# Shorter memory runs, weight reloads one step earlier, and another spread of the second batch's norm stages in a cross-attention and mixture-of-experts kernel

## The chip, the cores and the metric

The kernel runs on one core of one Trainium2 chip. The metric is the time of one execution on the device in microseconds (us). An execution is one launch that computes the whole block for four batches.

The core has a matrix engine (TensorE, in the profile PE for its matmuls and PEld for its weight loads), three engines for elementwise work (VectorE, in the profile DVE; ScalarE, ACT; GpSimd, POOL) and SyncE (SP), which in this kernel only issues data transfers. Transfers (DMAs) are issued on two queues here: those of SP, and those of POOL. Both are carried by the same 16 DMA engines. Each engine works through its own list of instructions in order, so an instruction that waits holds back whatever stands behind it on its engine.

## The reference

Inputs are `x` (4 batches, 512 rows, 512 features) and a context of 256 features for each row. Cut to what matters, and for each batch:

```
ln  = layernorm(x)
att = softmax((ctx Wq + bq)(ctx Wk + bk)^T)          # 512 x 512
x1  = x + (ln^T att)^T                               # cross attention
hs  = layernorm(x1)                                  # input of the block, and its residual
h   = rmsnorm(hs) * ln1
for 16 heads of 128: q, k, v = h wq, h wk, h wv
    a = softmax(q k^T / sqrt(128), causal) v
x2  = hs + concat(a) wo
t   = rmsnorm(x2) * ln2
top 6 of 16 experts for each row, weights from softmax(t gate^T)
out = x1 + x2 + sum over the 6 experts(silu(t eg) * (t eu)) ed + shared expert(t)
```

Each expert is 352 wide, the shared expert 704. All is float32. The kernel keeps the accuracy by splitting each float32 operand into two half-precision parts (a high one and a low one) and doing three half-precision matmuls for each product.

## The kernel before

**Cross attention** of a batch is written as a Python generator, `xattn(b)`. It yields after each small stage, and `step(b, n)` lets it run `n` stages on. There are 21 stages for batches 1 to 3: one for the two projections, eight for the energies and their softmax (two for each of four row tiles), and three for each of four row tiles that multiply the attention with the normalized input (`xm`, a group of 12 matmuls), normalize twice, and put the result transposed into `hT[b]`. These last twelve are the *norm stages*. The transposes are done by DMAs that SP issues (`flip`, line 91); in this document such a DMA is called a flip.

**Self attention** runs over a list of (batch, head) pairs, 64 in all, one head a step (the loop over `n`). The list goes through groups of two heads; from the third group on, batch 0 and batch 1 alternate with the same group (later batch 1 with 2, and 2 with 3), so that one set of weights serves two batches. In a step the queries and keys of a head are computed (`queries`), every second step also the values of its group (`values`), then the scores and their softmax (`scores`), and for the head of the step before the product with the values (`attend`, matmuls named `av`). `attend` reads a tile `pt` that four flips fill. `project` multiplies a finished group with its part of the output weights. The first batch is prepared ahead of the loop, and the first nine stages of batch 1 too. The twelve norm stages of batch 1 are done two a step in steps 0 to 5, and batches 2 and 3 are brought later by one or two stages a step. The first head of batch 1 stands at step 6.

**Weights.** `fetch` brings the weights of a head (`wqk`) or group (`wv`, `wo`), 512 KB each in split form. The first time, float32 weights are loaded into a staging tile, split by ScalarE and VectorE (`split`, lines 73 and 74), and the split form is written to a scratch tensor in memory (`wqk_d` and so on, line 429). Later uses load it from there (line 414): these are the *reloads*, 40 in all, issued by POOL at the place in the program where the weights are used. Two buffers of each kind exist, and `held` keeps a tile for the partner batch that uses it next.

**Routing.** When a batch is finished, `route1` to `route3` compute its expert choice. Rows are then sent to memory by scatters (line 467), indirect DMAs of 256 KB on POOL, a few in each step. `pace` holds them back: it puts a one-element copy on POOL that reads what a previous step's `attend` made, and the scatters stand behind that copy.

**The order** of instructions on each engine is not the program's. A planner simulates the program with costs of its own and writes out a list for each engine. Manual dependencies (`after`) and `pin` fix parts of that order. A moved instruction can thus move others on all engines.

After the attention come the shared expert and the 16 experts; the change has no part of its own there, except that `residual` loads `r_d`, and that the shared weights and the padding rows are brought with other shapes.

**Memory layout.** A tile has 128 partitions. In the kernel before, each scratch tensor and each prepared input has the partition as its first index, so that one DMA moves for each partition one unbroken run: 4 KB for a weight, 2 KB for a row of `x1_d`, `hid_d` or `r_d` (8 KB where four rows are loaded at once).

Of the kernel before, what the change touches and what calls it, by code (L numbers as in the profile page):

```python
# [17 lines left out]
P = 128  # L18
# [29 lines left out]
PS = 4096.0  # L48
GS = 8.0
LAG = 1  # L50
MLAG = 2
# [4 lines left out]
def xattn_moe_block_kernel(ctx: ExitStack, tc: tile.TileContext, x, xT, ctxT, wqkx, bqk, ln1, ln2,  # L56
# [23 lines left out]
    def mm3(o, terms, start=True, stop=True, hold=None):  # L80
        n = len(terms)
        for j, (lh, ll, rh, rl) in enumerate(terms):
            ins = nc.tensor.matmul(o, lh, rh, start=start and j == 0, stop=False)  # L83
            if hold and j == 0:
                after(ins, hold)
            nc.tensor.matmul(o, lh, rl, start=False, stop=False)  # L86
            ins = nc.tensor.matmul(o, ll, rh, start=False, stop=stop and j == n - 1)  # L87
        return ins

    def flip(o, i):  # L90
# [40 lines left out]

    hid_d = [dram.tile([P, NT, D], F32, name=f"hid_d{b}") for b in range(B)]
    x1_d = [dram.tile([P, NT, D], F32, name=f"x1_d{b}") for b in range(B)]
    wqk_d = [dram.tile([P, 2048], F16, name=f"wqk_d{h}") for h in range(H)]
    wv_d = [dram.tile([P, 8 * GW], F16, name=f"wv_d{g}") for g in range(G)]
    wo_d = [dram.tile([P, 2 * HG * D], F16, name=f"wo_d{g}") for g in range(G)]
    xs_d = dram.tile([ROWS, 2 * D], F16, name="xs_d")
    r_d = [dram.tile([P, NT, D], F32, name=f"r_d{b}") for b in range(B)]
    y_d = dram.tile([OFFS[E], D], F32, name="y_d")
# [39 lines left out]
    def ctx_load(b):  # L179
        t = stg.tile([P, 1024], F32, tag="st", name="ct32").rearrange("p (c s) -> p c s", c=CC)  # L180
        feed(b).dma_start(t, ctxT[b])
        return t

# [20 lines left out]
    def xattn(b):  # L204
        ct32 = ctx_load(b) if b else ct0

        def turned(j):
            t = (stg if b else wg).tile([P, 1024], F32, tag="st" if b else "wo", name="xT32")
            feed(b).dma_start(t, xT[b, j])
            return t  # L210
# [5 lines left out]
        if b == 0:  # L216
            nc.sync.dma_start(ln1b, ln1.partition_broadcast(P))
            for nm, src in (("wqk0", wqk[0]), ("wv0", wv[0])):
                t = vp.tile([P, NT, 2, GW], F16, tag="vt", name=f"{nm}_st")
                early_st[nm] = t.rearrange("p t a d -> p (t a d)").bitcast(F32)  # L220
                nc.sync.dma_start(early_st[nm], src)
        ctp = ap_.tile([P, 2, CC, S], F16, tag="lnp", name="ctp")
# [109 lines left out]
        for t in range(NT):  # L332
# [5 lines left out]
            q = nc.gpsimd if b else nc.sync  # L338
            q.dma_start(x1_d[b][:, t, :], xv)
            st = asm.tile([P, 6], F32, name="st")  # L340
# [14 lines left out]
            if b >= 2:  # L355
                q.dma_start(hid_d[b][:, t, :], hd)
            if stop == "A":
# [36 lines left out]
    def shared_pool():  # L394
        actx.close()
        sp = ctx.enter_context(tc.tile_pool(name="sp", bufs=1, side="right", reuse_waits="tile"))
        shx["p"] = ctx.enter_context(tc.tile_pool(name="ac0", bufs=1, side="right", reuse_waits="tile"))
        shw = shx["w"] = sp.tile([P, 2, C * 2 * SI], F16, name="shw")
        sdw = shx["d"] = sp.tile([P, 2, 6 * D], F16, name="sdw")
        for j in range(0, C * 2 * SI, 1024):  # L400
            pieces.append((shw[:, :, j:min(j + 1024, C * 2 * SI)], sgu[:, j:min(j + 1024, C * 2 * SI)]))
        for j in range(0, 6 * D, 1024):
            pieces.append((sdw[:, :, j:j + 1024], sd[:, j:j + 1024]))

    held, partner, seen = {}, {}, set()

    def fetch(b, g, pool, tag, n, src, scr, nm):
        if held.get(nm, (None,))[0] == (b, g):
            return held.pop(nm)[1]
        w = pool.tile([P, 2, n], F16, tag=tag, name=f"{nm}_{b}")  # L410
        if (b, g) in partner:
            held[nm] = partner[b, g], w
        if nm in seen:
            nc.gpsimd.dma_start(w.rearrange("p a n -> p (a n)"), scr)
            return w
        seen.add(nm)
        first = nm in early_st
        if first:
            st_ = early_st[nm]
        else:  # L420
            st_ = stg.tile([P, 1024], F32, tag="st", name=f"{nm}_st")
            q = nc.sync if nm == "wqk1" else nc.gpsimd
            ins = q.dma_start(st_[:, :n], src)
            if nm == "wqk1":
                after(ins, zz["hT", 0])
        for j, ins in enumerate(split(w[:, 0], w[:, 1], st_[:, :n], WS)):
            if first:
                after(ins, zz["nb"] if j else zz["calm"][0])
        ins = (nc.sync if nm == "wqk0" else nc.gpsimd).dma_start(scr, w.rearrange("p a n -> p (a n)"))
        if nm != "wqk0":  # L430
            zz["pad"] = ins
        if nm == "wqk0":
            after(ins, zz["ptp", 0])
        return w
# [5 lines left out]
    def shared_weights():  # L440
# [6 lines left out]
        if pieces:  # L447
            dst, src = pieces.pop(0)
            n = src.shape[1]
            st_ = stg.tile([P, 1024], F32, tag="st", name="shst")[:, :n]  # L450
            pin(nc.gpsimd.dma_start(st_, src))
            loaded.append((dst, st_))
# [3 lines left out]
    def pace(src):  # L456
        ins = nc.gpsimd.tensor_copy(mark, src)
        if "rrs" in zz:
            after(ins, zz["rrs"])
        for s in scats:  # L460
# [18 lines left out]
    def pad_rows(e):  # L479
        r = e * T + CAP + 1 - 3 * HB  # L480
        dst = xs_d[r:r + 3 * HB, :].rearrange("r d -> (r d)").rearrange("(p a n) -> p a n", p=P, a=2)
        src = causal[:, :S - P].bitcast(F16).unsqueeze(1).to_broadcast([P, 2, 2 * (S - P)])
        after(nc.gpsimd.dma_start(dst, src), zz["pad"])

    def route1(b, x2):
# [20 lines left out]
        if b == B - 1:  # L506
            pace(h2p[0:1, D:D + 1])
            for t, x1t in enumerate(x1s):
                after(nc.gpsimd.tensor_tensor(x1t, x1t, x2[:, t, :], ALU.add), scats[0])
                nc.gpsimd.dma_start(r_d[b][:, t, :], x1t)  # L510

    x1s = []

    def last_residual(b):
        for t, (pool, tag) in enumerate([(he, "pn3"), (he, "pn3"), (xp, "x1t"), (xp, "h2")]):
            x1t = pool.tile([P, D], F32, tag=tag, name="x1t", **({} if pool is he else dict(bufs=1)))
            nc.gpsimd.dma_start(x1t, x1_d[b][:, t, :])
            x1s.append(x1t)
# [3 lines left out]
    def rest_step():  # L522
        if rest:
            b, t, x2 = rest.pop(0)
            x1t = xp.tile([P, D], F32, tag="x1t", name="x1t", bufs=1)
            ins = nc.gpsimd.dma_start(x1t, x1_d[b][:, t, :])
            for s in scats[-1:]:
                after(ins, s)
            nc.gpsimd.tensor_tensor(x1t, x1t, x2[:, t, :], ALU.add)
            nc.gpsimd.dma_start(r_d[b][:, t, :], x1t)  # L530

# [91 lines left out]
    def values(b, g):  # L623
        hb = hT[b]
        wvt = fetch(b, g, wg, "wv", C * GW, wv[g], wv_d[g], f"wv{g}").rearrange("p a (c d) -> p a c d", c=C)
        vt = vts[b, g] = vp.tile([P, NT, 2, GW], F16, tag="vt", name="vt")
# [10 lines left out]
    def queries(b, h):  # L637
        hb = hT[b]
        wt = fetch(b, h // HG, wp, "wqk", 1024, wqk[h], wqk_d[h], f"wqk{h}").rearrange("p l (a c d) -> p l a c d", a=2, c=C)
        qk = qks[b, h] = []  # L640
# [54 lines left out]
    def project(b, g):  # L695
        if b not in x2s:
            x2s[b] = x2p.tile([P, NT, D], F32, tag="x2", name="x2")
            nc.gpsimd.dma_start(x2s[b], hid_d[b])
        ao, x2 = aos[b, g], x2s[b]
        wot = fetch(b, g, wg, "wo", HG * D, wo[g], wo_d[g], f"wo{g}").rearrange("p a (c d) -> p a c d", c=HG)  # L700
        for t in range(NT):
# [7 lines left out]
    def residual(b):  # L709
        if b not in accs:  # L710
            pool = hpool if b else shx["p"]
            accs[b] = pool.tile([P, NT, D], F32, tag="hT", name=f"acc{b}")
            nc.sync.dma_start(accs[b], r_d[b])
        return accs[b]
# [65 lines left out]
    for n in range(NH + LAG + 1):  # L780
        if n < NH:
# [13 lines left out]
            for p in parts:  # L795
                for _ in p:
                    pass
        m = n - LAG
        if n == NH:
# [18 lines left out]
        if 0 <= m < NH:  # L818
            b, h = heads[m]
            attend(b, h)  # L820
            if h % HG == HG - 1:
                ready.append((b, h // HG))
        if n in agenda and n < NH:
            b = agenda[n]
# [12 lines left out]
        if n < 6:  # L837
            step(1, 2)
        else:
# [397 lines left out]
def host_layout(i):  # L1237
# [5 lines left out]
    r["x"] = f["x"]  # L1243
    r["xT"] = f["x"].transpose(0, 2, 1).reshape(B, 2, 2, P, S).transpose(0, 1, 3, 2, 4).reshape(B, 2, P, 2 * S)
    r["ctxT"] = f["ctx_1024"].transpose(0, 2, 1).reshape(B, CC, P, S).transpose(0, 2, 1, 3)
    r["wqkx"] = np.stack([_pc(f["L0_xattn_Wq"].T, CC), _pc(f["L0_xattn_Wk"].T, CC)], 1)
# [6 lines left out]
    for n in ("wqk", "wv", "wo"):  # L1253
        r[n] = r[n].reshape(r[n].shape[0], P, -1)
    r["gate"] = _pc(g("gate_w").T, C).reshape(P, C * E)
# [10 lines left out]
    cols.append(np.concatenate([sg[:, :, 5 * P:], su[:, :, 5 * P:]], 2).reshape(P, C * P))  # L1266
    r["sgu"] = np.concatenate(cols, 1)
    r["sd"] = _pc(np.pad(g("sd_w").T, ((0, 6 * P - SI), (0, 0))), 6).reshape(P, 6 * D)
    return {k: np.ascontiguousarray(v) for k, v in r.items()}
# [24 lines left out]
```

## Time and profile before

| what | us |
|---|---|
| median of 3 runs | 1773.08 |
| lowest and highest run | 1766.79 and 1774.21 |
| profiled execution | 1762.41 |
| its span, first to last instruction | 1760.7 |
| PE busy in it | 1708.6 (97%) |
| DVE, ACT, POOL busy | 1116.2, 829.3, 485.1 |

The mean clock granted to TensorE is 0.993 of full speed. A profile comes from one execution. In its rows a name like `wqk<-wqk_d` says what is written and what is read; L414 is line 414 of the kernel; `x20` is a count. A value in square brackets behind an instruction is the time for which its engine had been idle before it, and what released it. "Busy" of PE means that matmuls are in the array or on their way; they overlap, so the time from start to start is a better measure than the length of one.

### The profile page before, as it was taken

Reading aid. Unit: us, or ns where it says so; the run is one execution under the profiler, and the core shown is the slowest. Engines: PE = TensorE matmul, PEld = TensorE weight load, DVE = VectorE, ACT = ScalarE, POOL = GpSimd, SP = SyncE. Lnnn points to the kernel's source line nnn. Section 1 sums busy time; section 2 is a strip of 40 time slices with the busy share of each in tenths; the row PEclk is TensorE's granted clock in tenths of the full one; section 3 lists DMA queues with packets and bytes.
Section 4 is the critical chain, followed back from the end, with each engine's and each line's share of the span. In section 5 each row is a group of like instructions: output and inputs, shape, how many; then the busy total and the mean of one; then the engine's idle time right before and its main releaser. Section 6 shows DMA issues by size and latency. Waiting matters only on the chain. (4 is left out here: it accounts for less than half of the span.)

```text
span 1760.7 us, 27659 instructions
## 1 busy us (share of the span) xinstructions
PE 1708.6 (97%) x9919; PEld 932.9 (53%) x9919; DVE 1116.2 (63%) x2766; ACT 829.3 (47%) x1711; POOL 485.1 (28%) x614
## 2 busy tenths in 40 slices
PE   7899999999998999999999999999999999999998
PEld 3555556565654555556555544455555555555553
DVE  6787877787785676776667647544434344356755
ACT  4565655565643545454445422344544445444431
POOL 5524212240255242121113454300000000034654
PEclk9999999999999999999999999999999999999999
DMA  7787867575687787556547653755554546589866
GB/s 246 181 205 184 225 150 192 122 196 118 138 183 187 163 177 179 120 120 118 111 104 132 140 155 128 247 173 148 150 173 137 154 143 163 154 228 254 221 198 213
DMA packets 392212, 296.24 MB, mean 168 GB/s; under 512 B 334880, under 2 KB 335136, under 8 KB 391296
## 3 DMA queue, kind: packets, MB, share of 16 engines
q1 hardware_dynamic: 353360, 159.87, 39.9%
q0 software_dynamic: 38704, 134.51, 25.5%
q8 instruction: 80, 1.31, 0.3%
q14 instruction: 68, 0.56, 0.1%
HBM read 124.81 MB, written 88.94 MB: 121 GB/s over the span
## 5 line engine op out<-in xcount | busy, mean ns | idle before, releaser
L1169 POOL DMA_INDIRECT yg<-y_d,yrc x96 | 109.9, 1145 | 505.2 <-PE u L87 426.0
L673 ACT ACTIVATE pe<-pe,bnm 128x128 f32<-128x128 f32 (+3 forms) x256 | 142.5, 557 | 161.5 <-DVE bnm L671 161.3
L83 PE MATMUL qk<-hT,wqk 128*128 128x512 f16 (+1 forms) x520 | 196.4, 378 | 9.1 <-DMA wqk<-wqk_d 5.5
L86 PE MATMUL qk<-hT,wqk 128*128 128x512 f16 (+1 forms) x520 | 196.5, 378 | 0.0
L87 PE MATMUL qk<-hT,wqk 128*128 128x512 f16 (+1 forms) x520 | 196.3, 377 | 0.0
L74 DVE SCALAR_TENSOR_TENSOR pn<-pe,brc,pn 128x128 f16<-128x128 f32 (+3 forms) x256 | 148.1, 590 | 21.3 <-ACT pn L73 18.0
L671 DVE CUSTOM_DVE_ANT_0 pe<-sc,causal 128x128 f32<-128x128 f32 (+3 forms) x256 | 117.0, 485 | 66.9 <-PE sc L668 65.9
L73 ACT ACTIVATE pn<-pe,brc 128x128 f16<-128x128 f32 (+3 forms) x256 | 133.5, 553 | 34.1 <-ACT pe L673 17.8
L83 PE MATMUL v<-wv,hT 128*128 128x256 f16 x512 | 139.8, 273 | 0.9 <-DMA hT<-hh 0.9
L87 PE MATMUL v<-wv,hT 128*128 128x256 f16 x512 | 139.7, 273 | 0.0
L86 PE MATMUL v<-wv,hT 128*128 128x256 f16 x512 | 139.7, 273 | 0.0
L83 PE MATMUL g<-xT,wt 128*128 128x384 f16 (+2 forms) x384 | 127.3, 331 | 0.0
L86 PE MATMUL g<-xT,wt 128*128 128x384 f16 (+2 forms) x384 | 127.2, 331 | 0.0
L87 PE MATMUL g<-xT,wt 128*128 128x384 f16 (+2 forms) x384 | 127.2, 331 | 0.0
L1058 ACT ACTIVATE hT_e<-hf 128x384 f16<-128x384 f32 (+3 forms) x96 | 51.1, 532 | 133.6 <-DVE hf L1072 133.2
L83 PE MATMUL y<-dt,hT_e 128*128 128x512 f16 (+1 forms) x288 | 109.4, 380 | 0.0
L87 PE MATMUL y<-dt,hT_e 128*128 128x512 f16 (+1 forms) x288 | 108.9, 378 | 0.0
L86 PE MATMUL y<-dt,hT_e 128*128 128x512 f16 (+1 forms) x288 | 108.9, 378 | 0.0
L73 ACT ACTIVATE qkt<-qk 128x512 f16<-128x512 f32 x128 | 75.1, 587 | 70.7 <-PE qk L87 70.5
L705 DVE SCALAR_TENSOR_TENSOR x<-wo,x 128x512 f32<-128x512 f32 x128 | 87.2, 685 | 33.3 <-PE wo L87 32.9
L467 POOL DMA_INDIRECT xs_d<-h2p,slotu x96 | 98.7, 1028 | 28.3 <-issue 27.1
L74 DVE SCALAR_TENSOR_TENSOR qkt<-qk,qkt 128x512 f16<-128x512 f32 x128 | 87.5, 684 | 18.3 <-ACT qkt L73 15.2
(333 smaller groups left out, 4041.5 us busy)
## 6 DMA issues: line engine op xcount, KB each, us to landing
y_d<-yt SPq DMA_DIRECT2D x96, 256.0 KB, 2.8
est<-in_ew_dram SPq DMA_DIRECT2D x32, 704.0 KB, 6.2
est<-in_ed_dram SPq DMA_DIRECT2D x16, 768.0 KB, 4.7
wqk<-wqk_d POOLq DMA_DIRECT2D x20, 512.0 KB, 5.0
wqk_d<-wqk POOLq DMA_DIRECT2D x15, 512.0 KB, 4.0
wqk_st<-in_wqk_dram POOLq DMA_DIRECT2D x14, 512.0 KB, 6.4
xs_d<-causal POOLq DMA_DIRECT2D x16, 384.0 KB, 5.6
wv<-wv_d POOLq DMA_DIRECT2D x10, 512.0 KB, 5.7
```

The costliest lines, as they stand in the source:

```text
L73: return (nc.scalar.activation(hi, src, AF.Copy, scale=scale), nc.vector.scalar_tensor_tensor(lo, src, scale, hi, ALU.mult, ALU.subtract))
L74: nc.vector.scalar_tensor_tensor(lo, src, scale, hi, ALU.mult, ALU.subtract))
L83: ins = nc.tensor.matmul(o, lh, rh, start=start and j == 0, stop=False)
L86: nc.tensor.matmul(o, lh, rl, start=False, stop=False)
L87: ins = nc.tensor.matmul(o, ll, rh, start=False, stop=stop and j == n - 1)
L467: ins = nc.gpsimd.indirect_dma_start(out=xs_d, out_offset=bass.IndirectOffsetOnAxis(ap=slotu[:, tt, k:k + 1], axis=0), in_=h2ps[tt], in_of ...
L671: nc.vector.tensor_tensor_reduce(pe, ps[:, :w], causal[:, S - w:], -1.0, 3e38, ALU.add, ALU.min, nm)
L673: nc.scalar.activation(pe, pe, AF.Exp, bias=nm, scale=-1.0, accum_out=sm)
L705: nc.vector.scalar_tensor_tensor(x2[:, t, :], ps, 1.0 / (VS * WS), x2[:, t, :], ALU.mult, ALU.add)
L1058: nc.scalar.activation(hT[:R, ic, :w], hf, AF.Copy)
L1169: nc.gpsimd.indirect_dma_start(out=yg, out_offset=None, in_=src, in_offset=bass.IndirectOffsetOnAxis(ap=idx[:, tt, k:k + 1], axis=0))
```

## The change

Three things change, and no arithmetic does.

1. *Runs.* A helper `runs` issues a DMA in blocks, and tensors in memory are laid out block first, then partition. Split weights are moved in runs of 1 KB (512 half-precision numbers), rows of `x1_d`, `hid_d` and `r_d` in runs of 1 KB (`RUN` = 256 float32 numbers), and staged weights and the transposed inputs in runs of 2 KB. The prepared inputs are laid out anew to match. The padding rows are written in 384 runs of 1 KB instead of 256 of 1.5 KB.
2. *Reloads.* `fetch` gets a mode `early`, which issues a reload and keeps the tile in `soon`. It is called for the next step's `wqk` and, where a group begins, `wv`, behind the queries of this step, and for `wo` behind the `attend` that finishes a group. A first load is not done early. `pace` puts its copy behind the last such reload on POOL.
3. *Norm stages.* In steps 0 to 5 `step(1, 2)` becomes `step(1, 3 * (n > 0))`: none in step 0, then three a step, so that the twelve are done by step 4.

The core of the diff (renamings and the other uses of `runs` are left out):

```diff
+RUN = 256
...
+    def runs(q, o, i):
+        blocks = [v.rearrange("p (q n) -> p q n", q=w.shape[0]) if len(v.shape) == 2 else v.rearrange("q p n -> p q n")
+                  for v, w in ((o, i), (i, o))]
+        return q.dma_start(*blocks)
...
-    hid_d = [dram.tile([P, NT, D], F32, name=f"hid_d{b}") for b in range(B)]
-    x1_d = [dram.tile([P, NT, D], F32, name=f"x1_d{b}") for b in range(B)]
-    wqk_d = [dram.tile([P, 2048], F16, name=f"wqk_d{h}") for h in range(H)]
+    def rows_d(nm, b):
+        return dram.tile([NT, D // RUN, P, RUN], F32, name=f"{nm}{b}")
+
+    def weights_d(nm, i):
+        return dram.tile([2048 // (2 * RUN), P, 2 * RUN], F16, name=f"{nm}{i}")
+
+    hid_d, x1_d, r_d = ([rows_d(nm, b) for b in range(B)] for nm in ("hid_d", "x1_d", "r_d"))
+    wqk_d = [weights_d("wqk_d", h) for h in range(H)]
...
+    def wqk_of(b, h, early=False):
+        return fetch(b, h // HG, wp, "wqk", 1024, wqk[h], wqk_d[h], f"wqk{h}", early)
...
-    def fetch(b, g, pool, tag, n, src, scr, nm):
+    def fetch(b, g, pool, tag, n, src, scr, nm, early=False):
+        if early and nm not in seen or soon.get(nm) and early:
+            return
         if held.get(nm, (None,))[0] == (b, g):
-            return held.pop(nm)[1]
-        w = pool.tile([P, 2, n], F16, tag=tag, name=f"{nm}_{b}")
+            return None if early else held.pop(nm)[1]
+        w = soon.pop(nm, None)
+        if w is None:
+            w = pool.tile([P, 2, n], F16, tag=tag, name=f"{nm}_{b}")
+            if nm in seen:
+                zz["load"] = runs(nc.gpsimd, w.rearrange("p a n -> p (a n)"), scr)
+        if early:
+            soon[nm] = w
+            return
         if (b, g) in partner:
             held[nm] = partner[b, g], w
         if nm in seen:
-            nc.gpsimd.dma_start(w.rearrange("p a n -> p (a n)"), scr)
             return w
...
     def pace(src):
         ins = nc.gpsimd.tensor_copy(mark, src)
-        if "rrs" in zz:
-            after(ins, zz["rrs"])
+        for k in ("rrs", "load"):
+            if k in zz:
+                after(ins, zz[k])
...
+            if n + 1 < NH:
+                b, h = heads[n + 1]
+                wqk_of(b, h, True)
+                if h % HG == 0:
+                    wv_of(b, h // HG, True)
...
             if h % HG == HG - 1:
                 ready.append((b, h // HG))
+                wo_of(b, h // HG, True)
...
         if n < 6:
-            step(1, 2)
+            step(1, 3 * (n > 0))
```

## The prediction

> **What bounds the kernel now.** The header and the first part of the page come first: TensorE is busy nearly all the time.
>
> ```profile
> span 1760.7 us, 27659 instructions
> PE 1708.6 (97%) x9919; PEld 932.9 (53%) x9919; DVE 1116.2 (63%) x2766; ACT 829.3 (47%) x1711; POOL 485.1 (28%) x614
> q1 hardware_dynamic: 353360, 159.87, 39.9%
> q0 software_dynamic: 38704, 134.51, 25.5%
> ```
>
> The timeline shows back-to-back 512-column matmuls starting every 0.215 us. Summing columns at that rate over all matmuls gives 1655 us; the rest of the span is pauses of PE, half-rate stretches after them, and small change. So nothing in this diff can win more than what PE waits for. The waits of PE say what that is:
>
> ```profile
> PE av L83 <- DMA pt<-pn: 16.9, 10, 3.9
> PE xm L83 <- DMA ptp<-pn: 9.8, 2, 5.8
> PE qk L83 <- DMA wqk<-wqk_d: 5.5, 1, 5.5
> PE qk L83 <- DMA hT<-hh: 3.6, 2, 3.2
> ```
>
> Columns: us in total, times, longest. Three rows are DMA transposes ("flips", issued by SP); one is a weight reload, once, 5.5 us. Its place, from the PE and POOL timelines:
>
> ```profile
> 538.93 0.96 POOL L467 DMA_INDIRECT xs_d<-h2p,slotu  x1 [0.30 <-issue]
> 539.89 0.60 POOL L414 DMA_DIRECT2D wqk<-wqk_d  x1
> ...
> 542.92 0.38 PE L668 MATMUL sc<-qkt,qkt 128*128 128x512 f16 x1
> 548.81 0.61 PE L83 MATMUL qk<-hT,wqk 128*128 128x512 f16 x1 [5.51 <-DMA wqk<-wqk_d]
> 549.21 0.63 PE L86 MATMUL qk<-hT,wqk 128*128 128x512 f16 x1
> 549.64 0.63 PE L87 MATMUL qk<-hT,wqk 128*128 128x512 f16 x1
> ```
>
> The reload was issued behind ten scatters of 256 KB, 3 us before its use. After the pause matmuls start 0.43 us apart until 554.0, i.e. at half rate for 5.2 us: 2.5 us more. The place costs **8.0 us**.
>
> **The change, part by part.** No matmul, activation or vector operation is added; counts are equal, order and DMA shapes differ.
>
> *Reloads a step ahead.* In the built order of POOL nearly all reloads keep their place within three instructions (wqk0, wqk1, wqk2, wqk9 and wqk11 move by one to three). One moves far: wqk3, the one above, from behind ten scatters to ahead of them and of the eight L611 multiplies, 17 to 20 us earlier (520 to 523). Its buffer was last read by the queries at 517.9 to 523, so POOL may hold up to 3 us there; behind it stand the L611 products and the scatters, for which nobody waits within the step. So wqk3 is there in time and the 5.5 us go. What is late next is a flip. In the new order PE does 4 matmuls with wqk3 and then `attend` (L83 av), which needs all four flips of its pt. They were issued here, and the issue view gives the landing:
>
> ```profile
> 537.82 1.58 SPq L91 DMA_TRANSPOSE pt<-pn  x1
> 539.80 1.43 SPq L91 DMA_TRANSPOSE pt<-pn  x1
> ...
> pt<-pn SPq DMA_TRANSPOSE x1, 9.3
> ```
>
> 9.3 us after 539.80 is 549.1: before the change `av` started at 550.92 and so never showed this wait. Now PE comes to it at 544.0. Upper bound of the pause: 5.1 us. But the reload's 512 KB no longer run beside this flip (8 rows of 4 KB per DMA engine, at some 0.16 us each in the input stream of 12 to 20 us: 1.3 us), and the flip itself is 64 packets per engine at 32 ns (from q1's 3424 packets in 61.5% of 11 us at 604 to 615): 2 us alone, so 2 us is the lower bound of its landing. I take a pause of 2 to 3 us.
>
> Here the clock decides. Row: after the 2.48 us pause at 585.43 the matmuls go on at 0.38 us (full rate), after 5.51 us they take 0.63. The Trainium skill, "TensorE: Matmul & The Clock Gate", Part 1, says that the clock halves after an idle window of about 3.4 us and needs about 3.4 us of work to return. It speaks against the change: a 4 us flip wait keeps the half rate. Then PE resumes at 548 and half rate till 553.2, a gain of 1 to 2 us; by the rule's recovery, 1.7 us of loss instead of the 2.5 measured, about 2.5. With a pause under 3.4 us the gain is 8.0 - 2 = **6.0 us**. I take 6.0; bounds 1 and 8.
>
> *Norm stages of batch 1.* `step(1, 2)` six times becomes nothing, then three at a time. The first xm of batch 1 leaves the place where PE waited 3.97 us at 72.4 to 76.6 (with the half rate after it 5.6 us). Next behind it in the new order are 6 scores matmuls, which need score banks that VectorE empties. VectorE and ScalarE stand in the same order as before up to there, and were held by the same flip:
>
> ```profile
> 71.89 0.72 ACT L73 ACTIVATE pn<-pm,rc 128x512 f16<-128x512 f32 x1 [4.63 <-DMA ptp<-pn]
> 72.64 0.75 DVE L74 SCALAR_TENSOR_TENSOR pn<-pm,rc,pn 128x512 f16<-128x512 f32 x1 [4.75 <-ACT pn L73]
> ...
> 74.78 0.55 DVE L671 CUSTOM_DVE_ANT_0 pe<-sc,causal 128x384 f32<-128x384 f32 x1
> ```
>
> The bank is free at 75.3 instead of 76.6: 1.3 us; work moved in front of `av` (14 qk and 9 sc matmuls, 4 us, against 12 xm, 2.6) cannot all be used, as wqk3's split ends at 81.3. I take **1.5 us**; bounds 0 and 5.6. The last batch-1 stage is a step earlier by count, but in the PE order its fourth xm stands 10 us ahead of the first batch-1 queries as before, so the 0.39 us hT wait at 138.9 is worth at most **0.5**. SP issues the same flips: the first two hT1 flips now stand behind four more pt flips of 1.3 us each, the third two places earlier; on POOL the first x1_d store of batch 1 stands behind six weight DMAs (3.5 us). Nobody on PE waits for either before the hT wait named.
>
> *Short runs.* Weight scratch (31 stores, 40 reloads) goes from 128 rows of 4 KB to 512 of 1 KB; staged inputs to 256 of 2 KB; x1, hid, r rows to 256 of 1 KB. POOL's price by form:
>
> ```profile
> L483 POOL DMA_DIRECT2D xs_d<-causal x16 | 11.7, 768 | 0.0
> L414 POOL DMA_DIRECT2D wqk<-wqk_d x20 | 11.0, 551 | 58.1 <-PE qk L87 56.6 <-PE rk L597 1.5
> L215 POOL DMA_DIRECT2D xt<-in_x_dram x2 | 1.6, 812 | 0.3 <-POOL x L354 0.3
> ```
>
> These are 256, 128 and 512 rows. So +0.26 us for each of 71 scratch DMAs, +0.2 for some 100 others: 40 us on an engine busy 485 of 1760, hidden by its idle time; without that cover, at a scatter burst, 0.5 us.
>
> The DMA engines: "DMA: Bandwidth & Descriptors", section "Why small descriptors are slow (HBM only)", gives about 3 cycles over 32-byte beats for each packet: 4 KB is 131 cycles, four 1 KB 140, +7%. The row: 993 packets of mean 2.5 KB in the input stream took 107 ns, 1384 of mean 2.3 KB, 299 of them flips' 256 bytes, 96 ns; split, this is about 163 ns for 4 KB and 88 for 2 KB, +8% already at 2 KB, and an estimated +23% at 1 KB. 71 x 1.3 us x 23% is 21 us of all engines, by the rule 6.5. It shows only where a flip or a load is waited for. First 25 us: 3.7 MB of input in 2 KB rows instead of 4, at saturated engines, +0.7 us on PE. Ten pt pauses and the flips around 67 us: 0.2 to 0.3 us each where scratch traffic runs beside, 2. In the other direction finer runs may let a flip alternate with 1 KB instead of 4 KB; but 256 rows of 2 KB (x1t and r_d, 604 to 615) appear as 160 packets, so rows are joined up to 4 KB and I count this little. Bounds -6 (flip waits a fifth shorter) to +12 (every pause of 31 us a third longer, some loads late); I take **+1.0** net.
>
> *Redrawn pauses.* Order on PE changes nearly everywhere to the end of attention. Pauses at 585, 643, 672, 921, 970 came with a load beside the flip; a load issued sooner takes up to 1.3 us off. I take -2 for all, bounds -6 and +6.
>
> **Sum**: -6.0 - 1.5 - 0.5 + 1.0 - 2.0 = -9.0. The profiled execution took 1762.4 (span 1760.7), the runs 1766.8 to 1774.2 with median 1773.1, 0.6% above it. I carry the difference over: **1764**.
>
> **Rivals.** (1) *The flip takes the reload's place*: pause of 4 to 5 us at 544, half rate stays. For it: 9.3 us of landing. Gain there 1.5, all in all -3.5, with runs at +2.5: 1771, no change to be told. (2) *Short runs make it slower*: in the first 600 us DMA share reaches 1.04 (80 to 100), flips are waited for by ScalarE (4.63 us above) and PE. If scratch and staging rows take a third longer, each of the 15 flip pauses (31 us) grows by 1 us or more, and staged weights, waited for by ScalarE 1.3 us at 87.9, hold its queue at some ten of 31 loads by 0.5: +17 against -6 gained, 1784. It decides once a 512 KB reload lands over 2 us later than now (5.0). Against it: half the DMA time is idle. (3) *Flips alternate per run*: flip waits a fifth shorter, -6 more: 1757. (4) The reload doesn't move is ruled out by the built order.
>
> **How the numbers follow.** Measurement tells about 0.5% (8.9 us) from no change. Stated sum and rival 3 together 0.42 (0.30 and 0.12), rival 1 0.27, rival 2 and worse 0.31. Faster 0.42, same 0.27, slower 0.31. Likeliest case alone: 1757 to 1769. Range for 8 in 10: 1750 to 1787; below it rival 3 with all bounds, above it rival 2 with POOL late too.
>
> **What would show it.** Right: no PE wait on wqk_d; at the first wqk3 queries of batch 1 a pt wait under 3.4 us and matmuls at 0.38 after it; first xm of batch 1 without a wait; reload issue near 0.81 us. Wrong: a pt wait of 4 us or more there with 0.63 after it; pt waits in total well over 17 us; reload landing over 7 us; DMA share of queue 0 over 30%.

## The result

The changed kernel takes 1787.14 us (median of 6 runs, 1783.68 to 1791.12), the kernel before 1768.12 us (6 runs, 1753.30 to 1774.21). The ratio is 1.0114 with a 95% interval of 1.0086 to 1.0141: **slower by 1.1%, some 20 us**, where 0.5% faster (1764) was forecast. Each ratio in this document is to executions of the kernel before that were timed in the same series. Their median lay between 1762.7 and 1769.6 us from one series to another, so below the ratios are compared and not the medians; a ratio is also not exactly the quotient of two medians.

The page of the changed kernel, header, engines and DMA queues:

```profile
span 1789.3 us, 27664 instructions
...
PE 1719.4 (96%) x9919; PEld 934.5 (52%) x9919; DVE 1121.1 (63%) x2766; ACT 828.1 (46%) x1711; POOL 517.5 (29%) x614
...
q1 hardware_dynamic: 358992, 159.87, 39.7%
q0 software_dynamic: 38960, 134.51, 25.0%
```

The work is the same and the DMA engines are no busier: POOL's queue (q0) takes 25.0% of their time against 25.5% before, and its packets grew from 38704 to 38960 only. POOL is busy 32 us more. What grew is what PE waits for:

```profile
PE av L84 <- DMA pt<-pn: 28.4, 10, 9.6
PE xm L84 <- DMA ptp<-pn: 6.6, 1, 6.6
PE qk L84 <- DMA hT<-hh: 5.8, 2, 3.9
PE u L1115 <- DVE hf L1106: 5.6, 2, 5.3
PE sc L694 <- ACT pm L325: 3.4, 1, 3.4
```

Columns as before: us in total, times, longest. The wait for `wqk_d` is gone (5.5 us). Waits for the flips of `pt` rose from 16.9 to 28.4 us, and one of them is 9.6 us long. Its place, in the changed kernel's SP, POOL and PE timelines:

```profile
591.46 0.37 SPq L94 DMA_DIRECT2D acc<-r_d  x1
592.00 8.40 SPq L97 DMA_TRANSPOSE pt<-pn  x4
...
594.30 0.75 POOL L94 DMA_DIRECT2D wqk<-wqk_d  x1 [4.68 <-PE qk L88]
...
596.24 1.08 POOL L495 DMA_INDIRECT xs_d<-h2p,slotu  x1 [0.18 <-issue]
597.62 1.02 POOL L495 DMA_INDIRECT xs_d<-h2p,slotu  x1 [0.30 <-issue]
598.95 0.97 POOL L495 DMA_INDIRECT xs_d<-h2p,slotu  x1 [0.30 <-issue]
600.22 0.97 POOL L495 DMA_INDIRECT xs_d<-h2p,slotu  x1 [0.30 <-issue]
...
611.73 0.61 PE L84 MATMUL av<-pt,vt 128*128 128x512 f16 x1 [9.61 <-DMA pt<-pn]
```

SP issues a 1 MB load (`acc`, line 741 of the changed kernel's `residual`) and right behind it the four flips that the next `av` needs; a reload and four scatters follow on POOL. `av` goes on 20.3 us after the load was issued, when the fourth flip has landed. This is the second `attend` behind the one at the old `wqk3` wait, and the reload here is that of `wqk4`. The kernel before has the same load ahead of the same four flips, and lost 2.5 us there:

```profile
570.46 0.34 SPq L713 DMA_DIRECT2D acc<-r_d  x1
570.95 7.92 SPq L91 DMA_TRANSPOSE pt<-pn  x4
...
575.35 0.54 POOL L414 DMA_DIRECT2D wqk<-wqk_d  x1 [4.92 <-PE qk L87]
...
585.43 0.39 PE L83 MATMUL av<-pt,vt 128*128 128x512 f16 x1 [2.48 <-DMA pt<-pn]
```

Adding up, over all of PE's timeline, each gap between two starts above what 2400 columns a microsecond need gives 91 us lost before and 121 after: 30 us, about the difference of the two profiled spans (28.6). That is more than the 19 us between the medians, since the profiled execution of the kernel before was 5.7 us under its median and that of the changed kernel 4.0 us over its own; the parts below are those of these two executions. The largest, with the half rate behind a pause: +8.7 at the place just shown; +6.5 at 247 us (scores behind ScalarE's `pm`); +5.7 at 414 us and +4 at 190 us (flips); +4.9 at 133 us (`hT` of batch 1); +3.6 at 1645 us. Gained: 8.2 at the old reload wait and 5.6 at the first `xm` of batch 1.

### The profile page after: what moved, and what is told of

It reads as the page before. It is cut to its first block, busy times and chain, and to the rows that moved or that the text cites. A ratio compares the mean times of both kernels' runs of the same rounds, so it can differ in the third digit from the quotient of the medians.

```text
span 1789.3 us, 27664 instructions
## 1 busy us (share of the span) xinstructions
PE 1719.4 (96%) x9919; PEld 934.5 (52%) x9919; DVE 1121.1 (63%) x2766; ACT 828.1 (46%) x1711; POOL 517.5 (29%) x614
## 3 DMA queue, kind: packets, MB, share of 16 engines
q0 software_dynamic: 38960, 134.51, 25.0%
## 5 line engine op out<-in xcount | busy, mean ns | idle before, releaser
L84 PE MATMUL av<-pt,vt 128*128 128x512 f16 (+3 forms) x256 | 78.2, 306 | 31.2 <-DMA pt<-pn 28.4
```

## The experiments

The change has three parts: reloads, norm stages, runs. In what follows, "places differ" counts how many entries of an engine's built list are not the same instruction as in another kernel's list, position by position; names of buffers and line numbers are left out.

The edits are shown in short: a comment behind a line names the runs that have it, and the lines that only carry it through the program are left out.

### One part at a time

**e1**, the reload edit put on the kernel before:

```diff
+            if n + 1 < NH:
+                b, h = heads[n + 1]
+                wqk_of(b, h, True)
+                if h % HG == 0:
+                    wv_of(b, h // HG, True)
...
+                wo_of(b, h // HG, True)
```

> The kernel before with the reload edit alone (early calls, the soon tile, the pace behind the last reload). Prediction's step: the wqk3 reload leaves its place behind ten scatters, no wait of PE on wqk_d, 6 us faster (1762). Rival: the built lists of all five engines are those of the kernel before, instruction for instruction, so the planner places reloads by its own due times whatever the program's place; then 1768 within 0.3% and the wait of about 5 us on wqk_d is still there.

Measured: 1767.40 us, ratio 0.9986 (0.9962 to 1.0009). The wait is there as before. The row of PE's waits in e1:

```profile
PE qk L83 <- DMA wqk<-wqk_d: 7.8, 1, 7.8
```

And POOL's timeline in e1, ahead of that wait:

```profile
537.04 1.32 POOL L485 DMA_INDIRECT xs_d<-h2p,slotu  x1 [0.30 <-issue]
538.67 0.96 POOL L485 DMA_INDIRECT xs_d<-h2p,slotu  x1 [0.31 <-issue]
539.63 0.59 POOL L425 DMA_DIRECT2D wqk<-wqk_d  x1
```

The reload stands behind the scatters still. **The edit moves nothing**: no place differs on any of the five engines from the kernel before.

**e2**, the norm stages alone:

```diff
-            step(1, 2)
+            step(1, 3 * (n > 0))
```

> The kernel before with only the norm stages changed (none in step 0, then three a step). Prediction's step: 2 us faster (1766). Theory N (the norm stages bring the loss: hT of batch 1 later, flips and ScalarE crowded between 100 and 260 us): 15 to 20 us slower (1783 to 1788), with a qk wait on hT of 3 us or more near 133 us. Theory R (short runs bring it): within 3 us of before. In its built order wqk3 is already ahead of the scatters, so either way there is no wait on wqk_d if that order is what removed it.

Measured: 1760.66 us, ratio 0.9970 (0.9947 to 0.9993): slightly faster, and faster than both kernels of the case. It is this edit that moves the `wqk3` reload ahead of the scatters: in e2 POOL's timeline reads

```profile
540.00 0.60 POOL L414 DMA_DIRECT2D wqk<-wqk_d  x1
540.62 1.88 POOL L611 TENSOR_TENSOR w<-oh,gpr 128x96 f32<-128x96 f32 x4
542.69 1.13 POOL L467 DMA_INDIRECT xs_d<-h2p,slotu  x1 [0.19 <-issue]
```

and none of the waits of PE is for `wqk_d`:

```profile
PE av L83 <- DMA pt<-pn: 12.2, 9, 3.2
PE qk L83 <- DMA hT<-hh: 8.8, 2, 5.5
PE xm L83 <- DMA ptp<-pn: 5.6, 1, 5.6
```

The hT wait of theory N is there (5.5 us at 140, with 2.3 of half rate), but not its 15 to 20 us. The profiled execution of e2 was one of its slowest (1771.43 us, 11 over the median): at equal work done it is 10 us behind the kernel before at 170 us of the span, 15 at 510, 2 at 680 and 8 at 1750.

**e3**, the runs alone (the changed kernel without the other two parts):

```diff
-            step(1, 3 * (n > 0))
+            step(1, 2)
...
-                wo_of(b, h // HG, True)
```

> The changed kernel with norm stages two a step and without the early reloads: short runs alone. Prediction's step: 1 us slower (1769). Theory R (short runs make flips land later, or hold POOL): 15 to 20 us slower (1783 to 1788), PE waits on pt 25 us or more in total. Theory N: within 3 us of before, pt waits about 17 us.

Measured: 1786.04 us, ratio 1.0100 (1.0063 to 1.0138). **e4**, the changed kernel without the reload edit:

> The changed kernel without the early reloads: short runs and norm stages together. If the reload edit moves nothing, the same as the changed kernel (1787, within 0.3%); if it gains 6 us, 1793; if it is what costs (crowding the flips behind the reload), 1770.

Measured: 1788.96 us, ratio 1.0108 (1.0038 to 1.0179), no place different from the changed kernel. So the runs bring the loss, about 1.0% alone and 1.4% on top of the norm stages. (The waits for `pt` in e3 are 22.0 us, and not 25 or more.)

### Which runs

**e5, e6, e7** put one kind of run on the kernel of e2; **e8** puts the scratch runs on the kernel before.

```diff
-    wqk_d = [dram.tile([P, 2048], F16, name=f"wqk_d{h}") for h in range(H)]
+    wqk_d = [dram.tile([4, P, 512], F16, name=f"wqk_d{h}") for h in range(H)]   # e7, e8; wv_d, wo_d alike
...
-    x1_d = [dram.tile([P, NT, D], F32, name=f"x1_d{b}") for b in range(B)]
+    x1_d = [dram.tile([NT, 2, P, 256], F32, name=f"x1_d{b}") for b in range(B)]   # e6; hid_d, r_d alike
...
-            ins = q.dma_start(st_[:, :n], src)
+            ins = runs(q, st_[:, :n], src)   # e5; all staged inputs alike
```

> Norm stages three a step, and of the short runs only the staged inputs and weights (256 rows of 2 KB instead of 128 of 4 KB). Its built lists are those of the kernel with the norm stages alone (1761), so any difference is the transfers' own. Theory shape (rows themselves cost): some of the 28 us between 1761 and 1789 is here, 1766 or more, since these are half of the bytes staged. Theory scratch (only the 1 KB scratch rows cost): 1761 within 0.3%.

> Norm stages three a step, and of the short runs only x1_d, hid_d and r_d (256 rows of 1 KB instead of 128 of 2 KB, and 1024 instead of 128 rows of 8 KB at the load of r_d and hid_d). Theory shape: 1766 or more, most of it at the flips behind the load of acc (near 600 us). Theory scratch: 1761 within 0.3%.

> Norm stages three a step, and of the short runs only the weight scratch (512 rows of 1 KB instead of 128 of 4 KB, 31 stores and 40 reloads). Its built order is near that of the changed kernel, 14 flips on SP stand otherwise than with the norm stages alone. Theory scratch: 1780 to 1789, pt waits of PE 25 us or more. Theory shape, spread over all three kinds: about a third of 28 us, 1770.

> Weight scratch in runs of 1 KB as the only change to the kernel before; flips on SP stand as before. Theory scratch, whatever the order: 1780 to 1787. Theory order (the planner's redrawn order costs, not the rows): 1768 within 0.3%, as SP's list is unchanged.

| run | median us | ratio | interval |
|---|---|---|---|
| e5 staged | 1770.27 | 1.0016 | 0.9992 to 1.0039 |
| e6 rows of x1, hid, r | 1764.98 | 0.9990 | 0.9959 to 1.0020 |
| e7 scratch | 1782.54 | 1.0090 | 1.0059 to 1.0121 |
| e8 scratch, without norm stages | 1777.72 | 1.0071 | 1.0049 to 1.0092 |

e6 gave what the theory of scratch says. e5 did not: 1770.27 us is what the theory of shape had asked for (1766 or more), 0.5% over e2 in the same order; but its interval reaches that of e2, and e9 below, with the same staged rows, does not repeat it. Weight scratch carries most of the loss, and in e7 the reload stands behind the scatters again (6.6 us of wait for `wqk_d`). That is not yet a cause, since scratch is also what redraws the order: in e5 no place differs from e2, in e7 3769 of PE, 48 of POOL and 14 of SP do. (e8 refutes the expectation that an unchanged SP list means an unchanged time; POOL differs in 13 places, PE in some 1400.) On the kernel before, rows and order are not told apart anywhere: e3 and e8 have both the rows and a redrawn order, though SP's list is the old one. What follows does it on the kernel of e2 alone.

### Rows or order

**e9** and **e12** have short rows in the order of e2. With `wqk` and `wv` scratch in 2 KB runs, and only `wo` in 1 KB, the planner keeps that order. **e10** takes e7's list and brings a partition's rows together in memory. **e11** has only `wqk` scratch in 1 KB.

```diff
-        return dram.tile([2048 // (2 * RUN), P, 2 * RUN], F16, name=f"{nm}{i}")
+        n = dict(wqk_d=1024, wv_d=1024, wo_d=512)[nm]   # e9, e12; e11: 512, 2048, 2048
+        return dram.tile([2048 // n, P, n], F16, name=f"{nm}{i}")
```
```diff
+        t = dram.tile([P, 4, 2 * RUN + 32], F16, name=f"{nm}{i}")   # e10
+        return t[:, :, :2 * RUN].rearrange("p q n -> q p n")
```

> Norm stages three a step; staged inputs and weights in 2 KB runs, scratch of wqk and wv in 2 KB runs, of wo in 1 KB. So nearly all of the short runs, but the built order is that of the norm stages alone (POOL, no row differs; SP 2; PE 30 of 29083). Theory shape (the rows themselves slow the transfers): 1778 to 1788. Theory order (the planner, which sees dearer transfers, redraws the order, and that costs): 1761 to 1770, what the staged inputs alone gave.

> As the scratch run with the norm stages (e7, 1782.5), same built order on all five engines, still 512 rows of 1 KB, but the four rows of a partition lie next to each other in memory (64 bytes apart) instead of 128 KB apart. If the distance of the rows in memory costs: 1761 to 1768. If it is the number of rows or the order: 1782 within 0.4%.

> Norm stages three a step; of all transfers only wqk scratch in 1 KB runs, everything else long. Its built order is near the redrawn one (POOL 14 and PE 1604 rows from the changed kernel, POOL 71 and PE 3915 from the norm stages alone). Theory order: 1778 to 1786. Theory shape: about half of the scratch loss, 1770.

> Norm stages three a step; only the weight scratch short, wqk and wv in 2 KB runs and wo in 1 KB, in the built order of the norm stages alone (POOL no row, SP 2, PE 30 of 29083 differ). Theory shape: 1770 to 1780. Theory order: 1761 within 0.3%.

| run | median us | ratio | interval |
|---|---|---|---|
| e9 | 1762.52 | 0.9982 | 0.9956 to 1.0007 |
| e10 | 1777.95 | 1.0052 | 1.0022 to 1.0083 |
| e11 | 1775.03 | 1.0035 | 1.0004 to 1.0067 |
| e12 | 1764.25 | 0.9953 | 0.9922 to 0.9983 |

e9 and e12 fit the theory of order. e10 does not decide: its interval meets e7's, and the distance of rows is at most a part. e11 lies between the two.

What was missing was 1 KB scratch in the old order, and the new order without the rows. Changing single weights shows that a 1 KB scratch of `wqk7` alone redraws thousands of places on PE, as do `wqk8` and `wv5`, while in e15 25 of the 32 weights are in 1 KB and the order stays that of e2.

```diff
+        n = 512 if nm == "wqk_d" and i in (7,) else 2048   # e13; e16: wqk_d 8; e14: wv_d 5
+        return dram.tile([2048 // n, P, n], F16, name=f"{nm}{i}")
```
```diff
+        n = 2048 if (nm, i) in (("wqk_d", 2), ("wqk_d", 7), ("wqk_d", 8), ("wqk_d", 10), ("wv_d", 3), ("wv_d", 4), ("wv_d", 5)) else 2 * RUN   # e15
```

> Norm stages three a step; of all memory layout only the scratch of one head's weights, wqk7, in 1 KB runs (one store, two reloads). The built order is nonetheless redrawn: 13 places of SP, 52 of POOL, 3869 of PE against the norm stages alone; against the changed kernel 4, 19 and 1950. Theory order: 1773 to 1787 (ratio 1.004 or more). Theory shape: as the norm stages alone, 1761 (ratio 0.997).

> Norm stages three a step; of all memory layout only the scratch of one group's weights, wv5, in 1 KB runs. Redrawn to yet another order: 12 places of SP, 41 of POOL, 2781 of PE against the norm stages alone, 10, 16 and 1343 against before. Theory order says only that it differs: anything from 1755 to 1790. Theory shape: 1761.

> Norm stages three a step; staged inputs and weights in 2 KB runs, pad rows in 1 KB, scratch in 1 KB runs for 12 of 16 wqk, 5 of 8 wv and all wo; the built order is that of the norm stages alone (POOL none, SP 2, ACT 4, PE 109 places differ). Theory order: 1761 to 1766 (ratio 1.000 or less). Theory shape: three quarters of the loss or more, 1779 or more.

> As the run with one head, but with wqk8 instead of wqk7: a third redrawn order (13 places of SP, 44 of POOL, 2739 of PE against the norm stages alone). Theory order: differs from 1761, by how much it does not say. Theory shape: 1761.

| run | short rows | order | median us | ratio | interval |
|---|---|---|---|---|---|
| e13 | 1 weight | redrawn | 1778.19 | 1.0110 | 1.0062 to 1.0159 |
| e14 | 1 weight | redrawn | 1762.69 | 1.0008 | 0.9974 to 1.0042 |
| e16 | 1 weight | redrawn | 1769.74 | 1.0043 | 1.0015 to 1.0071 |
| e15 | 25 of 32 weights, all staged, padding | of e2 | 1768.74 | 1.0034 | 0.9998 to 1.0070 |

**The order alone costs up to the whole loss**: e13 moves three DMAs in short rows and is, by the ratio, as slow as the changed kernel. How much depends on the order drawn; against e2's 0.9970 the three lost 1.4%, 0.4% and 0.7%. e14's loss is one that its interval does not part from none. e13 has only 4 runs (the quotient of its medians is 1.0088), and its profiled execution (span 1765.6) was well under its median, so that its trace does not show where its slower runs lose.

Rows in the old order (e5, e9, e12, e15) gave 1.0016, 0.9982, 0.9953 and 1.0034, a mean of 0.9996 against 0.9970: about 0.3%, 5 us, not parted from nothing in e9 and e12, and more likely something in e15, which met neither expectation (1.000 or less for order, 1779 us for shape). The rows of `x1_d`, `hid_d` and `r_d` are long in all four. Whether e15's 0.6% and e13's 1.4% add up is not settled: together they would be more than the 1.4% by which the changed kernel exceeds e2.

### One place in the order

In the orders of the changed kernel, e4, e7, e10, e11, e13, e14 and e16, and in those that rest on the kernel before too, SP issues the load of `acc` ahead of all four flips of head 33 (the fourth of batch 1); in e2, and in the runs with its order or nearly its order (e5, e6, e9, e12, e15), two of them go first. **e17** is the changed kernel, and **e18** the kernel of e13, with that load behind the four:

```diff
-            flip(pt[:, :2 * (t + 1), tl], pn)
+            zz["pt", b, h, t] = flip(pt[:, :2 * (t + 1), tl], pn)
...
-            runs(nc.sync, accs[b].rearrange("p t d -> p (t d)"), r_d[b].rearrange("t h p n -> (t h) p n"))
+            ins = runs(nc.sync, accs[b].rearrange("p t d -> p (t d)"), r_d[b].rearrange("t h p n -> (t h) p n"))
+            if b == 0:
+                after(ins, zz[("pt", *heads[33], NT - 1)])
```

> The changed kernel with one thing moved: the 1 MB load of acc (r_d of batch 0) on SP stands behind the four flips of one head instead of ahead of them (5 places of SP differ from the changed kernel, no other engine's order does). Theory place (of the redrawn order's cost a good part is the one pause near 600 us, where acc, the wqk3 reload and four scatters stand ahead of the flips): the pause of 9.8 us and its half rate shrink to 4 us or less in all, 1777 to 1781 (ratio 1.005 to 1.007). Rival (the reload and the scatters hold the flips, or the loss lies elsewhere): the pause stays over 7 us, 1787 (1.011).

> The run with one head's scratch in 1 KB (e13, ratio 1.011) with the load of acc behind the same four flips; 5 places of SP differ. Theory place: 1.004 to 1.007. Rival: 1.011, unchanged.

Measured: e17 1778.73 us, ratio **1.0043** (1.0012 to 1.0073), e18 1776.20 us, ratio 1.0028 (0.9998 to 1.0057). Neither interval meets that of its kernel without the move (1.0086 to 1.0141, and 1.0062 to 1.0159). Both gained somewhat more than expected. The medians of e13 and e18 are only 2 us apart, because the kernel before was slower in e18's series (1769.6 us against 1762.7). SP, POOL and PE of e17:

```profile
593.53 8.67 SPq L97 DMA_TRANSPOSE pt<-pn  x4
602.56 0.45 SPq L94 DMA_DIRECT2D acc<-r_d  x1
...
598.54 0.75 POOL L94 DMA_DIRECT2D wqk<-wqk_d  x1 [4.68 <-PE qk L88]
...
606.83 0.38 PE L84 MATMUL av<-pt,vt 128*128 128x512 f16 x1 [0.47 <-DMA pt<-pn]
```

The reload and the four scatters are there as in the changed kernel, and `av` waits 0.47 us instead of 9.61, at full rate. So **without the load ahead of the flips the pause is gone**, and the pause was 0.7% of the time, 12.6 us by the ratios, 11 by the trace. The reload did come later in e17, though: 5.0 us behind the first flip, against 2.3 in the changed kernel. The rest, 0.4%, is in this trace mostly at 190 us (6.8 us with half rate), 247 (4.6) and 415 (10.1), where the kernel before lost 2.1, nothing and 0.9; these places were not tried one by one.

Why the same load cost 2.5 us in the kernel before and 9.6 after was not tried, but the traces sort it in part. Twelve of the kernels have the load ahead of all four flips. In eight of them (before, e1, e3, e7, e8, e10, e11, e14) POOL issues the reload of `wqk4` 4.3 us or more behind the load, and the pause is 4.4 us at most. In the other four the reload, with the scatters behind it, comes 2.8 to 3.2 us behind the load, and the pause is 4.2 us (e13), 9.6 (the changed kernel), 10.0 (e16) and 11.1 (e4). So the long pause goes with both: a load ahead on SP and early traffic on POOL. No run keeps one and changes the other. The rows do not sort it (e16 loads `acc` in runs of 8 KB).

## Why the prediction was wrong

*Reloads a step ahead (−6.0).* **The attribution failed**: the edit that I credited does nothing (e1, e4), since the planner places a reload by its own account and not where the program names it. "One moves far: wqk3" was read from the order of the whole change, and what moved it was the norm stages (e2). e2's order holds all that these two parts do (−8.0 in the sum) and measured 0.3% less, 5 us (1 to 9), so the size was not what failed. Rival 4 was excluded by the same misreading: the reload did move, but not by its edit. The size at the place was right: no wait on `wqk_d`, and behind it a flip wait of 1.6 us at 566, against the 2 to 3 said, with the clock full.

*Norm stages (−1.5 and −0.5).* One step failed: hT of batch 1 was to be late by 0.39 us at most, "as before", because its `xm` stood ahead by 10 us (13 in the trace before, 12 after). The pause is 5.5 us in e2 and 3.9 in the changed kernel. SP and PE before, then after:

```profile
135.76 1.26 SPq L91 DMA_TRANSPOSE hT<-hh  x1
138.86 0.38 PE L83 MATMUL qk<-hT,wqk 128*128 128x512 f16 x1 [0.39 <-DMA hT<-hh]
...
130.61 2.36 SPq L97 DMA_TRANSPOSE hT<-hh  x1
137.41 0.58 PE L84 MATMUL qk<-hT,wqk 128*128 128x512 f16 x1 [3.87 <-DMA hT<-hh]
```

The last flip of hT was issued before PE came to it in both, but PE could go on 3.1 us behind that issue before and 6.8 after (8.4 in e2). The sum had taken this time as unchanged. The flip now stands 1.3 us behind a `pt` flip instead of 2.9; whether that or the loads on POOL's queue made it slow was not tried. The first `xm` lost its wait as said; in e2 3.1 us came back at once at the scores, in the changed kernel 3.0 us at an `av`.

*Short runs (+1.0, bounds −6 to +12).* The rows themselves cost about 5 us in e2's order, more than said and inside the bounds. POOL's price for a reload rose from 551 ns as forecast, to 767 instead of 812. In the changed kernel, by form:

```profile
L94 POOL DMA_DIRECT2D wqk<-wqk_d x20 | 15.3, 767 | 104.0 <-PE qk L88 96.0 <-issue 5.8 <-PE wo L88 2.2
```

From the cost per packet in the Trainium skill, "DMA: Bandwidth & Descriptors", section "Why small descriptors are slow (HBM only)", I had estimated +7% of engine time for 1 KB, and from my extrapolated row +23%. In the 10 us windows from 60 to 620 us in which both queues together held over 80% of the engines, POOL's queue took 53.2 us of engine time for a MB before and 50.0 in e2, 54.5 in e15 and 56.2 in the changed kernel: 2 to 12% more. Before and e2 have the same rows and differ by 6%, so this speaks against my 23% and cannot confirm the 7%. Nor could it: POOL's packets stayed at 38960 against 38704, so the trace shows the 1 KB rows joined, as said, and a cost per packet had hardly anything to act on. q0 stayed under 30%, as said.

*Redrawn pauses (−2, bounds −6 and +6).* **This is the step of the sum that failed.** I took a new order for a small change of chance, and for a gain because a load issued sooner takes its traffic from beside a flip. Orders redrawn with hardly a row changed cost 7 to 25 us against e2 (e14, e16, e13; 1, 8 and 19 us against the kernel before). The pause at 585 us was one of the five that this term was to shorten. In the changed kernel it is the 9.6 us pause instead, 8.7 us worse with its half rate, and moving one load behind four flips took 12.6 us off the kernel. The load stood ahead of these flips before too; that the pause there could grow, with the reload and the scatters sooner behind the load, was never priced. With 5 us gained in e2's order and 5 lost to the rows, some 20 us are left for this term, if the parts add up; the sum had allowed it 6 at most.

*The rivals.* Rival 2's number (1784) was near, but mainly for another reason: flips did wait longer (28.4 us in total against 16.9), yet short rows in the order of e2 cost some 0.6% in e15 and nothing clear in e9. What I held against rival 2 was misread: the queues' lines, 39.9% and 25.5%, leave a third of the DMA time idle and not half. Rival 1's mechanism, a flip that takes over with the half rate, came two heads later and twice as long (9.6 us).

*Smaller slips.* At 0.215 us for 512 columns the sum over all matmuls is 1673 us and not 1655, so pauses and half rate had less to give than it seemed. The flip waits shown are 14 with 30.3 us, not 15 with 31.

## What to carry to other kernels

Where a planner writes the order, an edit is to be built alone and its lists compared before any part of a gain is given to it: here one edit moved nothing, and another, the shape of three transfers, moved thousands of places. Read the new order of each DMA queue for a large transfer that now stands ahead of one that an engine waits for; here a dependency of two lines took that cost away. The orders drawn here with long rows, or with one weight short, lay from 0.3% under to 1.1% over the kernel before, so a layout is judged with the order held.

## What was not expected of the hardware

With a load of 1 MB issued 0.5 us ahead of the first flip, `av` could go on only 14.2 to 21.7 us after the load in the eleven kernels where it waited. In e17, with the load moved away, the 1.5 MB of reload and scatters that POOL issued behind the first flip left a wait of only 0.47 us.

What the half rate costs behind a pause did not follow the length of the pause: 1.4 us behind 3.9 (`hT`) and 1.6 behind 9.6 in the changed kernel, 2.5 behind 5.5 in the kernel before, 2.0 behind 7.8 in e1. The record of the granted clock shows why. These are the stretch at half clock behind the `wqk3` wait before, and the one behind the 9.6 us pause after; the first number behind the times is the length, the next is what PE was busy, and 0.50 is the granted clock:

```profile
547.20:554.00 6.80, 5.19 (x16) 2.24 (x17) 0.00 (x0) 0.00 (x0) 1.94 (x2) 0.50 0.90 293
604.60:614.80 10.20, 3.07 (x10) 1.46 (x11) 0.27 (x1) 0.00 (x0) 0.00 (x0) 0.50 0.81 119
```

PE works in the first for 5.19 us and in the second for 3.07, and loses half of that, 2.6 and 1.5 us. In all 20 traces the changes of the clock within a trace lie whole multiples of 3.41 us apart, so the cost depends on where in such a step PE comes back. The prediction had taken a pause under 3.4 us as safe for the clock. In these traces it is not: the clock stayed full behind 2.98 us (changed kernel, 84 us) and was halved from 198.5 to 201.9 us behind 2.04 us (e13, PE back at 197.5).
